# Four graph layers in one kernel: how the first layer is planned beside an eigenvector computation, and how the second layer's instructions are kept in order

## The chip, the cores and the metric

The kernel runs on one NeuronCore of a Trainium2 chip. The metric is the device time of one execution in microseconds (us). Times are medians of several runs; the profile is one execution more, whose own time is given beside it. The engines that matter are TensorE (PE, matmuls; PEld is its weight load), VectorE (DVE), ScalarE (ACT) and SyncE (SP), which issues the DMAs.

## What is computed

`x` has 128 graphs of 64 nodes with 256 features; `adj` is one 64 x 64 adjacency matrix. Each of four layers computes `h = relu(layernorm(x))` and adds the layer's output to `x`:

```python
# layer 0: h mixed with the normalized adjacency, two products, a batchnorm over all rows after each
agg = einsum('nm,bmd->bnd', A_hat, h)
t   = relu(batchnorm(agg @ W1.T + b1))          # 512 wide
x   = x + batchnorm(t @ W2.T + b2)              # 256 wide
# layer 1: the same with the eigenvectors of the normalized Laplacian
_, U = eigh(L_norm)
agg  = einsum('mn,bnd->bmd', U.T, h)
x    = x + einsum('nm,bmd->bnd', U, relu(agg @ W1 + b1) @ W2 + b2)
# layer 2: two graph convolutions with adj, then LSTMs over windows of 1, 2, 3 and 4 nodes
# layer 3: attention along 512 edges with a softmax per source node
```

Layers 2 and 3 are not touched by the change.

## The kernel before

**Tiles.** The 8192 rows of `x` lie in 16 blocks `X0` to `X15` of 512 rows each (128 partitions x 4 x 256). A block's layer norm takes four BATCH_NORM_STATS2, a short chain of small DVE operations with one square root on ACT, and four ACT activations (relu with scale and bias).

**Layer 0 beside the eigenvectors.** Layer 1 needs the eigenvectors `U` of a 64 x 64 matrix. They come from one long chain of small operations: 62 Householder steps that bring the matrix to tridiagonal form (`Fast.tridiagonal`, `Fast.householder`, one step per column c = 63 down to 2), then `Fast.vectors` (eigenvalues by polynomials, twisted factorizations, a verdict whether the result is good). Layer 0 is independent of it and runs beside it. `Plan` decides the order: `chain` places a step of the long chain as soon as its inputs are there by the planner's costs; `beside` puts a step of layer 0 into a queue per engine, and `fill` places queued steps in the time that an engine waits for the next chain step, if they fit with a little slack (0.6 us on T, 0.3 on S and V, for TensorE, ScalarE and VectorE). `emit` then issues all in the planned order, and with `nc.ordered` each instruction is tied behind the one before it on its engine (class `Ordered`; the ties cost no semaphores). What is not tied is put in order by the framework's own list scheduler, by its estimates, and it can be moved across a long stretch of the program.

**Layer 0's steps** (`hidden0`, `hidden_block`, `features0`). For each block: norm, relu (4 on ACT), two mixes (8 matmuls each with the block-diagonal `BDH`, tile `z`), eight products with W1 into four PSUM banks; each bank is read twice, by a BATCH_NORM_STATS2 into `st` and by an ACT copy that keeps the hidden values. When all 16 blocks are through, four BATCH_NORM_AGGREGATE (`bn_mv`) and a chain of small operations (`affine`) give scale and shift. Then for each block four ACT relus (tile `z`), eight products with W2, an ACT copy with a sum (into `big`) and an ACT square with a sum. The sums give the second batchnorm (tiles `bn_a`, `bn_b`, `bn_sh`, `bn_sc`). The norms of blocks 0 to 3 are computed together as one chain of 16 statistics and 13 small operations (`norms`), and so on by fours. The first of them wait in the plan for `came`, four empty chain steps on T that stand for the arrival of X0 to X3.

**DMAs of the start.** SP issues, in this order: adj and its transpose, X0 to X15, the weights and biases of layer 1 (`weights1`, tiles `w`, `w_n`, `w_b`), W1 and W2 of layer 0 and its six vectors. Then each Householder step issues one small DMA that copies the row `f_x` into a row of `f_V` (in `row_uk`). `f_x` has four buffers; a step cannot write a buffer before that DMA of four steps ago has read it.

**From layer 0 to layer 1** (`eigenvectors`). After the plan: three block-diagonal matrices from `U`, its transpose and adj (`block_diagonal`; tiles `BDU`, `BDUT`, `BDA`); for blocks 0 and 1 `end0`, which applies the second batchnorm (two ACT activations on `big`), transposes (8 on PE, PSUM tiles `ps` or `pe`) and adds to X (two DVE additions); the norm factors of block 0 (`norm0`, tiles `n_st`, `n_mv`, `n_v`, `n_r`, `n_m`); then a value is loaded on every engine, and a conditional branch skips a slow eigenvector routine that runs only where the verdict is bad.

**Layer 1** (`layer1`). For each block i: `first` (16 matmul records and a DVE maximum, tile `g`), `second` of block i - 1 (two DVE additions `y`, one into X), `mixed_again` (8, an ACT copy), `mixed` of block i + 1 (16; the copies `a` by DVE and ACT), `end0` of block i + 3, the norm of block i + 2 (tile `h`). None of this is tied before the change. `N1` (tile `w_n`) is the negative of a bias, made once by a DVE operation.

The code below has the lines of the profile; most compute instructions carry line 799, as they are issued through `Ordered`, so the profile is read by the tiles' names.

Of the kernel before, what the change touches and what calls it, by code (L numbers as in the profile page):

```python
# [787 lines left out]
class Ordered:  # L788
# [6 lines left out]
    def __getattr__(self, name):  # L795
        method = getattr(self.engine, name)

        def call(*a, **kw):
            i = method(*a, **kw)  # L799
            behind = self.last if self.owner.ordered else self.hold  # L800
            if behind is not None:
                self.owner.tc.add_manual_dep(i.ins, behind.ins.name, mybir.DependencyInfo(
                    mybir.DependencyClass.NoSync, mybir.DependencyReason.DATA), reason="issue order")
            if self.hold is None:
                self.last = i
            return i

        return call


class Engines:
# [5 lines left out]

    def __getattr__(self, name):
        return getattr(self.nc, name)


class Step:
# [3 lines left out]
    def __init__(self, engine, emit, needs, busy, ready, bank):  # L826
        self.engine, self.emit, self.needs = engine, emit, needs
        self.busy, self.ready, self.bank = busy, ready, bank
        self.at = None


class Plan:
# [26 lines left out]
    def fill(self, engine, until):  # L859
        while True:  # L860
            best = None
            for x in self.queue[engine][:12]:
                at = self.start(x)
                if at is not None and at + x.busy <= until + self.slack[engine] and (best is None or at < best[0]):
                    best = at, x
            if best is None:
                return
            self.queue[engine].remove(best[1])
            self.place(best[1], best[0])
# [7 lines left out]
    def beside(self, engine, emit, needs=(), busy=0.1, ready=0.22, bank=None):  # L877
        x = Step(engine, emit, needs, busy, ready, bank)
        self.queue[engine].append(x)
        return x  # L880
# [14 lines left out]
class Fast:  # L895
# [7 lines left out]
    def __init__(self, tc, ctx, k):  # L903
        self.tc, self.nc, self.k = tc, k.nc, k
        self.o = Ops(k.nc)
        self.pool = ctx.enter_context(tc.tile_pool(name="fast", bufs=1))
        self.rows = ctx.enter_context(tc.tile_pool(name="fastr", bufs=3))
        self.ps = ctx.enter_context(tc.tile_pool(name="fastps", bufs=2, space=PSUM))
        self.psv = ctx.enter_context(tc.tile_pool(name="fastvps", bufs=1, space=PSUM))
        self.tiles = {}  # L910
# [74 lines left out]
    def tridiagonal(self, S, made, plan):  # L985
# [24 lines left out]
        def first():  # L1010
            x = now["x"] = self.rows.tile([64, 65], F32, name="f_x", bufs=4)
            o.copy(x[:, 0:63], now["p"][:, 0:63])
# [10 lines left out]
    def householder(self, c, now, go, row, h, rest, scalars, square):  # L1023
# [40 lines left out]
        def row_x():  # L1064
            now["x"] = self.rows.tile([64, 65], F32, name="f_x", bufs=4)
            o.stt(x(0, w), now["uk"][:, 0:w], now["v"][:, w:c], now["z"][:, 0:w], ALU.mult, ALU.add)
# [123 lines left out]
    def values(self):  # L1190
# [5 lines left out]
        def signs(s):  # L1196
            if s % 4 == 3:
                SG = self.SG = self.rows.tile([128, 4, 64], F32, name="f_SG")
# [248 lines left out]
class Kernel:  # L1447
# [39 lines left out]
    def begin(self):  # L1487
# [9 lines left out]
        for i in range(NB):  # L1497
            self.X.append(self.c(f"X{i}", P, TPB, D))
            self.load_x(i)
# [5 lines left out]
    def block_diagonal(self, bd, M, psum):  # L1505

        p = psum.tile([P, N], F32, name="ps")
# [70 lines left out]
    def eigenvectors(self):  # L1578
# [3 lines left out]
        with ExitStack() as ex:  # L1582
# [10 lines left out]
            left = fast.vectors(self.U[:], self.UT[:])  # L1593
            plan.rest()
            plan.emit()
            for bd, M in ((self.BDU, self.U), (self.BDUT, self.UT), (self.BDA, self.AT)):
                self.block_diagonal(bd, M[:], self.ps0)
            for i in range(2):
                self.end0(i, self.ps0, "ps")
            self.norm0 = self.factors(self.w0, 0, self.const)  # L1600
            bad = nc.values_load(left[0:1, 0:1], min_val=0, max_val=64)
# [45 lines left out]
    def norms(self, pool, blocks):  # L1647
# [4 lines left out]
        st = pool.tile([P, n, 6], F32, name="m_st")  # L1652
        d, v, y, r, m = (pool.tile([P, n], F32, name="m_" + x) for x in "dvyrm")
# [50 lines left out]
    def affine(self, pool, tag, mean, var, b, g, be):  # L1704
# [5 lines left out]
            ("S", lambda: self.act(y[:], v[:], AF.Sqrt)),  # L1710
            ("V", lambda: o.recip(r[:], y[:])),
# [3 lines left out]
            ("V", lambda: o.ts(sc[:], r[:], 2.0, ALU.mult)),  # L1715
            ("V", lambda: o.mul(sc[:], sc[:], g[:])),
            ("V", lambda: o.add(v[:], mean, b[:])),
            ("V", lambda: o.sub(sh[:], b[:], v[:])),
# [22 lines left out]
    def open0(self, ctx):  # L1741
# [4 lines left out]
        self.W0 = self.weights(w, "w0_1", io["L0_gnn_W1_t"]), self.weights(w, "w0_2", io["L0_gnn_W2_t"])  # L1746
        self.v0 = [self.columns(w, "w0_" + n, io["L0_gnn_" + n]) for n in "b1 g1 be1 b2 g2 be2".split()]
        self.st1 = w.tile([P, 4, NB, 6], F32, name="st1")
        self.sums = w.tile([P, 2, 2, NB], F32, name="sums")

# [6 lines left out]
    def hidden0(self, plan, mixes):  # L1757

        nc, pool, psum, W1 = self.nc, self.p0, self.ps0, self.W0[0]
        beside, used, banks = plan.beside, {}, []  # L1760
        for i in range(NB):
            if i % 4 == 0:
                r, m, steps = self.norms(pool, range(i, i + 4))
                came = [plan.chain("T", lambda: None, (), 0.0, 5.5 + 1.5 * (i + k)) for k in range(4)] if i == 0 else []
                d = []
                for n, (engine, emit) in enumerate(steps):
                    if n < 4 * TPB:
                        d.append(beside("V", emit, [came[n // TPB]] if came else [], 0.36, 0.45))
                    else:
                        d = [beside(engine, emit, d, 0.12, 0.25)]  # L1770
                normed = d
            banks += self.hidden_block(i, r, m, plan, normed + used.get(i - 3, []) + [mixes], used)
        self.features0(plan, banks, used)

    def hidden_block(self, i, r, m, plan, needs, used):
# [3 lines left out]
        def relu(j):  # L1779
            if j == 0:  # L1780
                now["z"] = pool.tile([P, 4, BT], F32, name="z", bufs=3)
                now["h"] = now["z"][:, 0:2, :].rearrange("p c (t d) -> p (c t) d", d=D)
            self.act(now["h"][:, j, :], self.X[i][:, j, :], AF.Relu, scale=r[:, i % 4, j:j + 1],
                     bias=m[:, i % 4, j:j + 1])
# [20 lines left out]
        for hc in range(4):  # L1805
# [5 lines left out]
                               0.62, 0.7))  # L1811
# [5 lines left out]
    def features0(self, plan, made, used):  # L1817
# [7 lines left out]
        def sequence(steps, d):  # L1825
            for engine, emit in steps:
                d = [beside(engine, emit, d, 0.12, 0.25)]
# [3 lines left out]
        d = [beside("V", lambda j=j: nc.vector.bn_aggr(mv[:, j, :], flat(self.st1[:, j, :, :])), made, 0.5, 0.65)  # L1831
# [66 lines left out]
    def end0(self, i, psum, name="pe"):  # L1898

        sc2, sh2 = self.affine2  # L1900
        for oc in range(2):
            self.act(self.part(i, oc), self.part(i, oc), AF.Identity, scale=sc2[:, oc:oc + 1], bias=sh2[:, oc:oc + 1])
        self.add_transposed(psum, i, lambda dc, j: self.part(i, dc)[:, j * P:(j + 1) * P], name)
# [22 lines left out]
    def layer1(self, pool, psum, ps2, ps0, tables, after):  # L1926
        o = self.o
        (W1, W2), N1, b1, T = self.W1, self.N1, self.b1, self.T1

# [32 lines left out]
        mixed(0)  # L1962
        self.end0(2, ps0)
        hs[1] = self.norm(pool, 1)
        o.ts(N1[:], N1[:], -1.0, ALU.mult)
        for i in range(NB + 1):
# [20 lines left out]
            if i + 2 < NB:  # L1987
                hs[i + 2] = self.norm(pool, i + 2)
            if i == NB - 1:
                after()  # L1990
# [34 lines left out]
    def layer2(self, pool, psum, ps2, ps0):  # L2025
# [26 lines left out]
        def block(i):  # L2052
            if i == 2:
                with ExitStack() as ce:
                    epool = ce.enter_context(self.tc.tile_pool(name="l3e", bufs=1, side="right"))
                    nc.vector.hold, nc.scalar.hold, nc.tensor.hold = nc.vector.last, nc.scalar.last, nc.tensor.last
                    self.edges(self.w3, epool, ps0)
                    nc.vector.hold = nc.scalar.hold = nc.tensor.hold = None
# [476 lines left out]
    def run(self):  # L2535
# [4 lines left out]
        with cx:  # L2540
            self.big = [pool.tile([P, 2, 4 * BT], F32, name="big") for pool in pools]
            with ExitStack() as ex:
                self.weights1(ex.enter_context(self.tc.tile_pool(name="l1c", bufs=1)))
# [47 lines left out]
```

## Time and profile before

| | us |
|---|---|
| median of three runs | 2362.17 (2361.97 to 2363.38) |
| the profiled execution, its own time | 2361.27 |
| its span from the first to the last instruction | 2359.5 |
| stage of layer 0 and the eigenvectors, to the start of the second batchnorm's chain | 0 to 388.9 |
| from there to the first relu of layer 1 | 388.9 to 405.4 |
| layer 1, to the first mix of layer 2 | 405.4 to 519.6 |
| layers 2 and 3 | 519.6 to 2359.5 |

Engines over the whole span: PE 97% busy, DVE 68%, ACT 48%. The busy shares are sums of instruction durations; neighbouring DVE or ACT instructions overlap a little, and PE's ends are modelled, so PE can be shown busy while it runs at half its clock. A timeline line gives the start, the duration, engine, operation, output and inputs, and, in brackets, how long the engine was idle before and for whom.

### The profile page before, as it was taken

What the parts mean: (1) busy time and instruction counts of PE and PEld (TensorE: products, weight loads), DVE (VectorE), ACT (ScalarE), POOL (GpSimd) and SP (SyncE); (2) the same over time, 40 slices, a digit from 0 to 9 for tenths busy, and PEclk for the clock granted to TensorE, in tenths of its full rate; (3) what the DMA queues carried; (4) which work ended last, traced back from release to release, by engine and by line L of the source; (5) the groups of instructions that cost most, each with busy time, mean ns of one, the idle gap of its engine ahead of it and who ended that gap; (6) DMA issues with size and microseconds to landing.
All of it is one profiled execution on the core that took longest, in us unless ns stands there. A gap on an engine that the chain in (4) does not pass through costs nothing.

```text
span 2359.5 us, 32444 instructions
## 1 busy us (share of the span) xinstructions
PE 2281.3 (97%) x12061; PEld 1618.5 (69%) x12061; DVE 1603.2 (68%) x4045; ACT 1134.5 (48%) x2488; POOL 2.9 (0%) x26
## 2 busy tenths in 40 slices
PE   5998997999999999999999999999999999999989
PEld 3554344997777788888999998888884444444434
DVE  5887675999437786666777676559655566556467
ACT  4665766544436654434444444336445544344321
POOL 0000000000000000000000000000000000000000
PEclk9999999999999999999999999999999999999989
DMA  5000221131010000000000002000020000000001
GB/s 169 1 1 1 63 63 36 65 81 36 1 36 1 1 18 1 1 1 32 6 1 1 1 1 72 1 1 16 1 63 10 1 5 19 14 14 19 14 14 50
DMA packets 61194, 54.88 MB, mean 23 GB/s; under 512 B 15203, under 2 KB 58852, under 8 KB 61028
## 3 DMA queue, kind: packets, MB, share of 16 engines
q1 hardware_dynamic: 61028, 52.73, 7.3%
q8 instruction: 97, 1.59, 0.3%
q14 instruction: 69, 0.57, 0.1%
HBM read 35.93 MB, written 16.78 MB: 22 GB/s over the span
## 4 chain that ended last, share of the span: by engine, by line
PE 78%; DVE 3%; ACT 1%; issue 1%; DMA 0%; ACTq 0%; DVEq 0%
PE ps L799 68%; PE acc L799 5%; PE pt L799 4%; PE y L799 1%; PE pe L799 1%; DVE sm_m L799 1%; DVE X L799 1%; ACT ls_g L799 0%; ACT big L799 0%; DVE aw L799 0%; ACT L799 0%; DVE n_st L799 0%; DMA ls_w<-in_L_gnn_Wih_t_dram 0%; ACT h L799 0%; DVE sm_e L799 0%
## 5 line engine op out<-in xcount | busy, mean ns | idle before, releaser
L799 ACT ACTIVATE ls_g<-ls_g,ls_b 128x512 f32<-128x512 f32 (+4 forms) x472 | 243.0, 565 | 153.6 <-DVE ls_g L799 151.8
L799 ACT ACTIVATE ls_g<-ps,ls_b 128x256 f32<-128x256 f32 (+3 forms) x268 | 115.3, 470 | 329.7 <-PE ps L799 326.5
L799 PE MATMUL ps<-z,w 128*128 128x512 f32 x512 | 256.1, 627 | 0.0
L799 PE MATMUL ps<-big,X 128*128 128x176 f32 (+3 forms) x848 | 212.9, 367 | 1.6 <-ACT big L799 1.5
L799 DVE TENSOR_TENSOR aw<-at,ed_OST 128x1024 f32<-128x1024 f32 x128 | 150.0, 1219 | 92.4 <-PE ps L799 92.4
L799 DVE TENSOR_TENSOR ls_g<-ls_z,ps 128x512 f32<-128x512 f32 (+5 forms) x256 | 146.8, 579 | 90.8 <-PE ps L799 89.3
L799 PE MATMUL ps<-ls_tx,X 128*128 128x160 f32 (+2 forms) x960 | 206.9, 327 | 0.6 <-ACT ls_g L799 0.6
L799 PE MATMUL ps<-X,X 128*128 128x160 f32 (+1 forms) x896 | 199.0, 306 | 0.0
L799 PE MATMUL ps<-X,ls_w 128*128 128x256 f32 x640 | 190.5, 379 | 0.0
L799 PEld LDWEIGHTS ps<-ls_tx,X 128*128 128x128 f32 x960 | 161.8, 190 | 15.0 <-DVE X L799 4.7
L799 PEld LDWEIGHTS ps<-big,X 128*128 128x128 f32 x848 | 146.0, 190 | 31.4 <-issue 19.4
L799 DVE TENSOR_TENSOR X<-ls_g 128x1024 f32<-128x1024 f32 (+2 forms) x108 | 117.4, 1087 | 50.5 <-ACT ls_g L799 50.4
L799 ACT ACTIVATE r<-ps 128x512 f32<-128x512 f32 x256 | 129.3, 625 | 41.1 <-PE ps L799 41.0
L799 PEld LDWEIGHTS ps<-X,X 128*128 128x128 f32 x896 | 148.5, 190 | 0.0
L799 PE MATMUL ps<-X,ls_s 128*128 128x256 f32 x480 | 142.3, 379 | 0.0
L799 PEld LDWEIGHTS ps<-z,w 128*128 128x128 f32 x512 | 89.2, 193 | 72.9 <-issue 64.6
L799 PE MATMUL ps<-ls_tx,ls_s 128*128 128x256 f32 x464 | 134.8, 379 | 0.0
L799 PE MATMUL ps<-ls_tx,ls_w 128*128 128x256 f32 x464 | 133.4, 380 | 0.1
L799 PEld LDWEIGHTS ps<-X,ls_w 128*128 128x128 f32 x640 | 121.6, 190 | 16.6 <-DVE X L799 0.3
L799 PE MATMUL ps<-big,ls_w 128*128 128x256 f32 x464 | 132.0, 380 | 0.7 <-ACT ls_z L799 0.7
L799 PE MATMUL ps<-ed_S,Q 64*128 64x512 f32 x512 | 128.6, 617 | 0.5 <-DVE XV L799 0.3
L799 ACT ACTIVATE big<-ps 128x512 f32<-128x512 f32 x96 | 69.2, 749 | 113.8 <-PE ps L799 113.6
(534 smaller groups left out, 4024.3 us busy)
## 6 DMA issues: line engine op xcount, KB each, us to landing
X<-in_x_dram SPq DMA_DIRECT2D x32, 512.0 KB
xs<-X SPq DMA_DIRECT2D x16, 512.0 KB
X<-xs SPq DMA_DIRECT2D x16, 512.0 KB
out_dram<-X SPq DMA_DIRECT2D x32, 256.0 KB
X<-in_L_gnn_Wih_t_dram SPq DMA_DIRECT2D x4, 512.0 KB
ls_w<-in_L_gnn_Wih_t_dram SPq DMA_DIRECT2D x4, 512.0 KB
ls_w<-in_L_gnn_Whh_t_dram SPq DMA_DIRECT2D x4, 512.0 KB
w<-in_L_gnn_W_t_dram SPq DMA_DIRECT2D x2, 512.0 KB
```

The lines of the kernel that those rows point to most:

```text
L799: i = method(*a, **kw)
```

## The change

It touches the stage of layer 0 and the eigenvectors, the passage to layer 1, and the order in layer 1.

- **DMAs.** X0 is loaded first, then layer 0's W1, X1 to X15, W2 and the vectors; layer 1's constants come last of the loads.
- **Block 0's norm by itself.** The norms are computed for blocks 0, 1 to 3, and then by fours. `came` is now an `event` with a time of its own instead of a chain step on T. The steps of block 0's norm are `urgent`: `fill` prefers such a step and places it as soon as it could start before the next chain step, whether it fits or not.
- **Batchnorm chains.** The first batchnorm's statistics of blocks 14 and 15, its aggregates and its chain are urgent; `affine` has one operation fewer, and two are moved beside the square root.
- **Buffers.** `f_x` has eight buffers; the pool's other tiles two in place of three.
- **Passage.** The block-diagonal matrices are emitted before the rest of the plan, in another PSUM tile; the value is loaded before the second batchnorm is applied; the scalings of blocks 0 and 1, the transposes and `norm0` are tied in an order with `norm0` ahead of block 1's additions.
- **Layer 1.** Everything up to the end of its first iteration is tied in program order (the negation of N1 too). After that, instructions of an iteration are only held behind what was last on their engine when the iteration before began.

```diff
 class Engines:
+    def fresh(self):
+        for e in (self.tensor, self.vector, self.scalar):
+            e.last = None
+    def mark(self):
+        return [e.last for e in (self.tensor, self.vector, self.scalar)]
+    def hold(self, marks=(None, None, None)):
+        for e, last in zip((self.tensor, self.vector, self.scalar), marks):
+            e.hold = last
...
     def fill(self, engine, until):
...
-                if at is not None and at + x.busy <= until + self.slack[engine] and (best is None or at < best[0]):
-                    best = at, x
+                if at is not None and (at + x.busy <= until + self.slack[engine] or x.urgent and at <= until):
+                    if best is None or (not x.urgent, at) < best[:2]:
+                        best = not x.urgent, at, x
...
+    def event(self, at):
+        x = Step(None, None, (), 0.0, at, None)
+        x.at = 0.0
         return x
...
-        self.rows = ctx.enter_context(tc.tile_pool(name="fastr", bufs=3))
+        self.rows = ctx.enter_context(tc.tile_pool(name="fastr", bufs=2))
...
-            x = now["x"] = self.rows.tile([64, 65], F32, name="f_x", bufs=4)
+            x = now["x"] = self.rows.tile([64, 65], F32, name="f_x", bufs=8)
...
             self.X.append(self.c(f"X{i}", P, TPB, D))
-            self.load_x(i)
+        self.load_x(0)
...
             left = fast.vectors(self.U[:], self.UT[:])
+            for bd, M in ((self.BDA, self.AT), (self.BDU, self.U), (self.BDUT, self.UT)):
+                self.block_diagonal(bd, M[:], fast.psv, "fvps")
             plan.rest()
             plan.emit()
-            for bd, M in ((self.BDU, self.U), (self.BDUT, self.UT), (self.BDA, self.AT)):
-                self.block_diagonal(bd, M[:], self.ps0)
+            bad = nc.values_load(left[0:1, 0:1], min_val=0, max_val=64)
+            nc.ordered = True
             for i in range(2):
-                self.end0(i, self.ps0, "ps")
-            self.norm0 = self.factors(self.w0, 0, self.const)
-            bad = nc.values_load(left[0:1, 0:1], min_val=0, max_val=64)
+                self.features1(i)
+            for i in range(2):
+                self.add_transposed(self.ps0, i, lambda dc, j, i=i: self.part(i, dc)[:, j * P:(j + 1) * P], "ps")
+                if i == 0:
+                    self.norm0 = self.factors(self.w0, 0, self.const)
+            nc.ordered = False
+        nc.fresh()
...
             ("S", lambda: self.act(y[:], v[:], AF.Sqrt)),
+            ("V", lambda: o.add(sh[:], mean, b[:])),
+            ("V", lambda: o.sub(sh[:], b[:], sh[:])),
...
-            ("V", lambda: o.ts(sc[:], r[:], 2.0, ALU.mult)),
-            ("V", lambda: o.mul(sc[:], sc[:], g[:])),
-            ("V", lambda: o.add(v[:], mean, b[:])),
-            ("V", lambda: o.sub(sh[:], b[:], v[:])),
+            ("V", lambda: o.stt(sc[:], r[:], 2.0, g[:], ALU.mult, ALU.mult)),
...
-        self.W0 = self.weights(w, "w0_1", io["L0_gnn_W1_t"]), self.weights(w, "w0_2", io["L0_gnn_W2_t"])
+        W1 = self.weights(w, "w0_1", io["L0_gnn_W1_t"])
+        for i in range(1, NB):
+            self.load_x(i)
+        self.W0 = W1, self.weights(w, "w0_2", io["L0_gnn_W2_t"])
...
+        self.weights1(self.consts1)
...
     def hidden0(self, plan, mixes):
-                r, m, steps = self.norms(pool, range(i, i + 4))
-                came = [plan.chain("T", lambda: None, (), 0.0, 5.5 + 1.5 * (i + k)) for k in range(4)] if i == 0 else []
+        for lo, hi in ((0, 1), (1, 4), (4, 8), (8, 12), (12, 16)):
+            r, m, steps = self.norms(pool, range(lo, hi))
+            came = [plan.event(4.5 + 1.5 * (i + (i > 0))) for i in range(lo, min(hi, 4))]
...
+                    d.append(plan.beside(engine, emit, [came[n // TPB]] if came else [], 0.36, 0.45, urgent=not lo))
+                else:
+                    d = [plan.beside(engine, emit, d, 0.12, 0.25, urgent=not lo)]
...
             bank.append(beside("V", lambda hc=hc: nc.vector.bn_stats(self.st1[:, hc, i, :], now["p", hc][:]), [x],
-                               0.62, 0.7))
+                               0.62, 0.7, urgent=i >= NB - 2))
...
-                d = [beside(engine, emit, d, 0.12, 0.25)]
+                d = [beside(engine, emit, d, 0.12, 0.25, urgent=True)]
...
     def layer1(self, pool, psum, ps2, ps0, tables, after):
+        nc.fresh()
+        nc.ordered = True
...
         mixed(0)
+        o.ts(N1[:], N1[:], -1.0, ALU.mult)
         self.end0(2, ps0)
         hs[1] = self.norm(pool, 1)
-        o.ts(N1[:], N1[:], -1.0, ALU.mult)
+        marks = nc.mark()
         for i in range(NB + 1):
...
+            nc.ordered = False
+            nc.hold(marks)
+            marks = nc.mark()
             if i == NB - 1:
+                nc.hold()
                 after()
```

## Prediction, made before the change was built or run

> **What bounds the kernel now.** I read the windows first: busy time of each engine by stretch (start:end, length, then PE, PEld, DVE, ACT, POOL with instruction counts, PE clock, DMA share, GB/s).
>
> ```profile
> 12.00:38.00 26.00, 7.06 (x40) 5.67 (x40) 14.74 (x81) 7.45 (x33) 0.00 (x0) 1.00 0.90 271
> 38.00:227.00 189.00, 185.45 (x859) 97.49 (x857) 148.54 (x727) 124.70 (x425) 0.00 (x0) 1.00 0.01 1
> 227.00:240.60 13.60, 3.34 (x36) 2.67 (x36) 12.14 (x71) 5.39 (x28) 0.00 (x0) 0.62 0.01 1
> 279.00:370.00 91.00, 88.27 (x302) 39.57 (x302) 69.40 (x333) 60.30 (x147) 0.00 (x0) 1.00 0.19 55
> 406.50:520.00 113.50, 111.92 (x851) 105.15 (x850) 106.85 (x354) 62.03 (x126) 0.00 (x0) 1.00 0.22 68
> ```
>
> From 38 us on PE sets the pace of layer 0, except for a hole at 227 to 240.6; before 38 it is all but idle. In layer 1 PE and DVE are both full. So layer 0 gains by an earlier start of PE, a smaller hole, and a shorter passage to layer 1. The timeline says what holds the start, first on DVE, then on PE:
>
> ```profile
> 27.14 0.21 DVE L799 SCALAR_TENSOR_TENSOR f_junk<-f_uA,f_uk 64x60 f32<-64x60 f32 x1 [0.39 <-ACT f_uk L799]
> 30.43 0.23 DVE L799 TENSOR_SCALAR w_n<-w_n 128x128 f32<-128x128 f32 x1 [3.08 <-DMA w_n<-in_L_gnn_b_dram]
> 36.78 0.27 DVE L799 SCALAR_TENSOR_TENSOR f_x<-f_uk,f_v,f_z 64x59 f32<-64x59 f32 x1 [5.94 <-DMA f_V<-f_x]
> ...
> 31.54 2.08 PE L799 MATMUL ps<-BDH,z 128*128 128x128 f32 x8
> 38.15 2.07 PE L799 MATMUL ps<-BDH,z 128*128 128x128 f32 x8
> 40.73 2.08 PE L799 MATMUL ps<-z,w 128*128 128x512 f32 x2
> ```
>
> At step c = 60 DVE waits twice: for layer 1's bias, whose negation was put in here, and for an `f_x` buffer whose copying DMA stands in SP's queue behind all loads (SP issues the first at 34.78). PE's order is fixed, so the second mix stands behind the stalled step. Then the hole and the passage:
>
> ```profile
> 229.35 0.68 DVE L799 BATCH_NORM_STATS2 st<-ps 128x6 f32<-128x512 f32 x1
> 235.91 0.57 DVE L799 BATCH_NORM_AGGREGATE bn_mv<-st 128x2 f32<-128x96 f32 x1
> 239.75 1.51 ACT L799 ACTIVATE z<-X,bn_sh,bn_sc 128x512 f32<-128x512 f32 x2
> 240.63 2.08 PE L799 MATMUL ps<-z,w 128*128 128x512 f32 x2
> ...
> 385.87 0.22 ACT L799 ACTIVATION_READ_ACCUMULATOR ps<-ps,bn_less 128x1 f32 x1
> 388.93 0.18 DVE L799 TENSOR_REDUCE bn_a<-sums 128x2 f32<-128x32 f32 x1 [2.96 <-DVEq L1602]
> 405.37 2.08 ACT L799 ACTIVATE h<-X,n_m,n_r 128x256 f32<-128x256 f32 x4
> ```
>
> The four aggregates come one per Householder step. After the last square DVE waits 2.96 us for its branch, and layer 1's first relu comes 16.4 us after the second batchnorm starts. The verdict itself was ready at 369.7 (CAST at 369.55), 14.5 us before PE's last product ended (384.24).
>
> [...] a mix takes 2.08 us at 31.54 and 1.16 at 214.11; after the hole the low clock lasts 6.4 us (0.50 in 240.6 to 247). [...] `f_v` waited behind the bias. [...] the branch itself is 0.07 us on DVE, but its next event comes 2.9 us later. I use 2.96.
>
> **The change, part by part**, against the profiled execution's 2361.27 us; the median is 0.90 above it.
>
> *The stall.* With N1's negation tied into layer 1 and eight buffers, both waits go: 3.08 + 5.94 and the two operations between, 36.78 - 27.35 = 9.4 us of the chain. What is late next: the ninth write of `f_x`, at c = 55, needs the DMA of c = 63. That still stands behind the same bytes (landing about 36.8), and c = 55 comes at about 50 (57.79 less about 7). Cover 13 us; if it is gone, it costs its excess. The pool's two buffers in place of three wait for readers one whole step back, so 0.
>
> *SP's queue.* The same loads in another order. W1 is now second behind X0; X1 to X3 move 0.5 MB back, 1.5 us at about 330 GB/s. Layer 1's constants go last; they are needed after 360. Cost 0.
>
> *Block 0's norm.* By the planner's own costs, the old `came` counts from when T is free (6.3 after the adjacency's steps): block 3 at 6.3 + 5.5 + 4.5 = 16.3, four statistics 1.9 and 13 operations of 0.25 bring the first relu to 21.5. It ran at 25.78, 4.3 later than planned; the first `f_x` was planned at 8.9 and ran at 11.25, 2.4 later. New: statistics from 6.7 in the chain's waits, ready at 8.9, 3.3 for the chain: 12.2, so really 14.6 to 16.5; I take 15. Relus need 3 us (25.78 to 28.6 before), so the first mix runs at about 17.5 in place of 31.54, and the first product at 22 in place of 40.73. I take **19 us** for PE's stream. Blocks 1 to 3 need 12 statistics and 13 operations; 16 and 13 took 11.3 us (14.39 to 25.7), so they are ready at about 23, before block 0's products end. Cost to the chain: four 0.34 and 12 of about 0.1, half of it in waits: 1.2 us.
>
> *The hole.* From the last hidden product (226.6) to 240.63: 14 us. With urgent steps: two statistics 1.4, four aggregates 2.2, eleven chain operations 2.4 and the root, one relu 0.8, woven with chain steps: 8. Gain **6 us**. `affine`'s fewer operation: 0.2, once in each batchnorm.
>
> *Where the two meet.* PE's last product: 384.2 - 19 - 6 = 359.2; but features now lie beside 14 Householder steps in place of 9, and each has about 0.9 us of its own matmuls: + 4.5 = 363.7. The chain: 369.7 - 9.4 + 1.2, and two steps that lay in the hole (3.3 us each) now lie under load (4.1): 1.6. Verdict at 363.1. They meet; squares end 1.9 after PE: 365.6; branch on DVE 363.1 + 3.0 = 366.1. So the second batchnorm starts at 366.1 in place of 388.9: **-22.8**, -23.0 with `affine`. On PE and ACT the branch lies in their remaining work; PE's branch took 3.5 us before without a gap in its matmuls. Bounds: 0 if ACT and PE carry their branches in the queue, + 3 if one is exposed. I take 0.
>
> *Passage.* Before, ACT ran 11 scalings and DVE 11 additions for blocks up to 7 ahead of block 0's relu. Tied: two scalings 1.55, transposes and two additions to + 3.9, statistics 1.4, aggregates 0.4, root and six operations 1.8: relu at + 7.5 after the batchnorm's chain, in place of 12.9 (405.37 - 392.49): **-5.4**.
>
> *Layer 1.* The work that ran ahead (5.5 blocks of transposes, 44 x 0.109 = 4.8 us of PE, 11 additions of 0.6 = 6.6 us of DVE) returns into a loop where both are full. Also in the tied first iteration `first` needs `a`, `mixed_again` needs `g`, and `g` stands on DVE behind block 1's norm (3.3 us), for which block 0's mix and PE wait. Less one block's, which stays ahead: **+ 5.4**, between 0 and + 9. The loop's pace was 7.0 us per block (113.5 / 16 = 7.1); a hold of one to two iterations still leaves the engines a block of freedom: 0, bounded by -3 (fewer waits at DVE) and + 8 (0.5 us a block).
>
> Sum: -23.0 - 5.4 + 5.4 = -23.0; 2361.27 - 23.0 = 2338.3, as a median **2339.2**.
>
> **Rivals.**
> *A, forecast: 2339* (2331 to 2347), 0.55.
> *B, the chain is the later one or PE starts less early: 2348.* If block 0's relu comes only where DVE's stall was (PE -9.4 us), the hole gives 3 and the branch 2.96 hides: -15 + 1 = -14. For: the plan's times are rough (2.4 to 4.3 us off already at the start), and loaded steps last 4.2 us against 3.3 unloaded. Against: X0 lands long before it is used. 0.17.
> *C, the passage is paid back less, or the hole shrinks more: 2331.* -5.4 stays and layer 1 costs 0, with 3 more from its DVE: -31. For: DVE is what layer 1 waits for at its end (relu waits of ACT for `n_m` of about 4 us a block). 0.16.
> *D, slower: layer 1's order costs more than the rest gains.* If, in the held iterations, `g` stands behind the norm of a later block on DVE as in the tied one, PE waits once per block. It decides from 23 / 15 = 1.5 us a block; at 2.2 us a block it is + 33: 2372. For: DVE has 106.85 busy us in 113.5, so a wait is not caught up. Against: only the first iteration is fully tied. 0.07.
> *E, the change doesn't do what it says: 2359.* The stall moves to the next wait (X, `f_V`) and PE starts where it did; only the branch gains. 0.05.
>
> **Numbers.** About 0.2%, 4.7 us, is what a measurement can tell from no change. Faster: A, B, C and nearly half of E: 0.90; within: 0.03; slower: D: 0.07. Range: from C's 2331 less 4 for its own spread to B's 2348 plus 5: 2327 to 2353; outside lie D, E and tails, 0.2.
>
> **What would show it.** No DVE wait for `w_n` or `f_V` before 60 us; the first mix at about 17.5; first features product at about 216; `bn_a` at about 366; first relu of layer 1 7.5 us after the batchnorm's chain; layer 1 from its first relu to layer 2's first mix 119 to 120 us in place of 114. Wrong if the verdict comes later than 368, if PE waits in 20 to 60 us, or if layer 1's blocks take more than 7.5 us.

## The result, and the profile after

| us | before | after |
|---|---|---|
| median of 16 runs | 2361.62 (2360.14 to 2363.38) | 2354.26 (2350.15 to 2358.75) |
| ratio, 95% interval | | 0.9971 [0.9964, 0.9979] |
| profiled execution, its own time | 2361.27 | 2354.39 |
| second batchnorm starts (`bn_a`) | 388.9 | 368.7 |
| its chain ends (`bn_sh`) | 392.5 | 375.5 |
| first relu of layer 1 (`h`) | 405.4 | 383.05 |
| first mix of layer 2, called the third layer below | 519.5 | 514.0 |
| from `bn_a` to that mix | 130.6 | 145.3 |

The kernel is 7.4 us faster; 23 were forecast, and the time lies 1.3 us above the stated range. By the two profiles the first stage gives 20.2 us, and the stretch from the second batchnorm to the third layer takes 14.7 of them back. The windows of the kernel after (start:end, length, then PE, PEld, DVE, ACT, POOL with counts, PE clock, DMA share, GB/s):

```profile
12.00:38.00 26.00, 21.95 (x99) 13.77 (x98) 21.78 (x114) 17.98 (x60) 0.00 (x0) 1.00 0.91 267
38.00:207.90 169.90, 166.39 (x775) 86.48 (x773) 134.30 (x653) 109.90 (x378) 0.00 (x0) 0.99 0.01 2
207.90:217.00 9.10, 1.91 (x22) 1.45 (x21) 7.49 (x44) 3.72 (x17) 0.00 (x0) 0.75 0.00 0
217.00:368.00 151.00, 147.16 (x513) 63.48 (x513) 102.00 (x537) 102.25 (x296) 0.00 (x0) 0.97 0.21 56
384.10:514.00 129.90, 123.02 (x888) 115.36 (x889) 112.14 (x365) 72.17 (x143) 0.00 (x0) 0.95 0.19 60
```

The first 26 us now hold 21.95 us of PE's work (7.06 before), and the hole is 9.1 us (13.6). In layer 1 DVE is busy 86% of its window, where it was 94%. The timeline after, at the places shown for before:

```profile
17.05 3.98 PE L799 MATMUL ps<-BDH,z 128*128 128x128 f32 x16 [0.58 <-ACT z L799]
22.20 4.56 PE L799 MATMUL ps<-z,w 128*128 128x512 f32 x10
...
209.57 0.57 DVE L799 BATCH_NORM_AGGREGATE bn_mv<-st 128x2 f32<-128x96 f32 x1
217.00 1.22 PE L799 MATMUL ps<-z,w 128*128 128x512 f32 x1 [0.76 <-ACT z L799]
...
369.89 0.17 DVE L799 TENSOR_SCALAR bn_b<-bn_b 128x2 f32<-128x2 f32 x1
373.69 0.17 DVE L799 TENSOR_SCALAR bn_v<-bn_b 128x2 f32<-128x2 f32 x1 [3.63 <-DVEq L1626]
...
383.05 2.07 ACT L799 ACTIVATE h<-X,n_m,n_r 128x256 f32<-128x256 f32 x4 [1.45 <-DVE n_m L799]
```

DVE has no wait for `w_n` or `f_V` before 60 us. The first product comes 18.5 us earlier, the first features product 23.6. But the jump over the slow eigenvector code, which stood ahead of `bn_a`, now stands inside the chain, between `bn_b` and `bn_v`: 3.63 us. The instructions of the conditional's line (count, shortest/median/longest ns, first and last start) say how long each engine jumps:

```profile
L1626 ACTq EVENT_SEMAPHORE  x2: 17/17/17, 371.8 to 371.9; - x2
L1626 DVEq EVENT_SEMAPHORE  x2: 21/21/21, 373.5 to 373.6; - x2
L1626 ACTq COMPARE_BRANCH  x1: 50/50/50, 368.9 to 368.9; - x1
L1626 PEldq COMPARE_BRANCH  x1: 4012/4012/4012, 368.9 to 368.9; - x1
L1626 DVEq COMPARE_BRANCH  x1: 72/72/72, 370.5 to 370.5; - x1
```

DVE branches at 370.5 in 72 ns and goes on at 373.5; ACT needs 2.9 us (368.9 to 371.8), PE 4.0. On DVE and ACT the branch record is the small part of it (72 and 50 ns) and a gap behind it the rest; on PE the record itself lasts 4012 ns.

**The loss in layer 1.** From the batchnorm's end to the third layer's first mix, one window of each kernel, before and after:

```profile
392.50:519.50 127.00, 121.81 (x904) 112.43 (x905) 117.38 (x382) 75.56 (x146) 0.74 (x3) 0.98 0.19 62
```
```profile
375.50:514.00 138.50, 126.60 (x904) 118.42 (x905) 117.50 (x384) 76.35 (x149) 0.74 (x3) 0.94 0.19 60
```

DVE (the third pair) has the same work, 117.4 and 117.5 us, and is idle 9.6 and 21.0 us. With equal work the idle time must grow by what the window grows, 11.4 us; what counts is where it lies. By windows inside it, 16 of the 21 us lie in the first 34.5 us, up to 410 (first before, then after):

```profile
392.50:406.50 14.00, 10.39 (x60) 7.78 (x61) 11.03 (x31) 13.99 (x22) 0.74 (x3) 0.82 0.02 5
406.50:420.00 13.50, 11.99 (x96) 11.35 (x95) 13.23 (x65) 13.17 (x26) 0.00 (x0) 1.00 0.16 22
```
```profile
375.50:384.10 8.60, 3.58 (x16) 3.06 (x17) 5.36 (x19) 4.18 (x8) 0.74 (x3) 0.70 0.28 66
384.10:396.00 11.90, 8.59 (x40) 7.84 (x40) 5.27 (x20) 3.49 (x8) 0.00 (x0) 0.61 0.15 24
396.00:410.00 14.00, 12.24 (x79) 11.45 (x80) 7.78 (x24) 6.62 (x12) 0.00 (x0) 0.88 0.00 0
```

PE falls behind as well: in its first 34.5 us it has 135 of its 904 matmuls, where it had 209 before, and from 430 us on it is busy without a gap (from 420 before, but for 0.1 us). So both engines enter the rest of the layer with work undone, and these lines don't tell which of the two sets its length. The timeline of the tied first pass shows what they wait for:

```profile
384.12 3.76 PE L799 MATMUL ps<-BDU,h 128*128 128x128 f32 x16 [3.94 <-ACT h L799]
386.26 0.69 DVE L799 COPY a<-ps 128x512 f32<-128x512 f32 x1 [2.24 <-PE ps L799]
387.92 0.60 ACT L799 ACTIVATE a<-ps 128x512 f32<-128x512 f32 x1 [2.79 <-PE ps L799]
388.41 1.51 ACT L799 ACTIVATE big<-big,bn_sh,bn_sc 128x512 f32<-128x512 f32 x2
389.27 0.47 PE L799 MATMUL pe<-ident,big 128*128 128x128 f32 x1 [1.39 <-ACT big L799]
390.91 0.69 DVE L799 TENSOR_TENSOR X<-X,pe 128x512 f32<-128x512 f32 x1 [3.82 <-PE pe L799]
...
395.63 0.68 DVE L799 TENSOR_TENSOR g<-ps,w_n 128x512 f32<-128x512 f32 x1
396.36 1.76 PE L799 MATMUL ps<-BDUT,g 128*128 128x128 f32 x8 [2.03 <-DVE g L799]
```

It is one chain: ACT scales block 2 only behind its copy `a`, which waits for the mix; PE waits for the scaling, DVE for PE's transposes (3.82 us), and then `g`, behind block 1's norm on DVE, keeps PE waiting (2.03).

### The profile page after: what moved, and what is told of

The parts are those of the page before. It is cut to its first block, busy times and chain, and to the rows that moved or that the text cites. A ratio compares the mean times of both kernels' runs of the same rounds, so it can differ in the third digit from the quotient of the medians.

```text
span 2352.6 us, 32457 instructions
## 1 busy us (share of the span) xinstructions
PE 2285.1 (97%) x12061; PEld 1620.8 (69%) x12061; DVE 1604.6 (68%) x4055; ACT 1134.0 (48%) x2489; POOL 3.0 (0%) x26
## 4 chain that ended last, share of the span: by engine, by line
PE 79%; DVE 3%; ACT 1%; issue 1%; ACTq 0%; DVEq 0%
PE ps L799 68%; PE acc L799 5%; PE pt L799 4%; PE pe L799 1%; PE y L799 1%; DVE X L799 1%; DVE sm_m L799 1%; ACT ls_g L799 0%; DVE n_st L799 0%; DVE aw L799 0%; ACT L799 0%; ACT big L799 0%; ACT h L799 0%; DVE sm_e L799 0%; DVE ls_g L799 0%
## 5 line engine op out<-in xcount | busy, mean ns | idle before, releaser
L799 DVE TENSOR_TENSOR X<-ls_g 128x1024 f32<-128x1024 f32 (+2 forms) x108 | 117.5, 1088 | 50.5 <-ACT ls_g L799 50.4
L799 PE MATMUL ps<-X,ls_s 128*128 128x256 f32 x480 | 142.3, 379 | 0.0
L799 ACT ACTIVATE h<-X,n_m,n_r 128x256 f32<-128x256 f32 x192 | 99.7, 589 | 45.8 <-DVE n_m L799 22.4
```

## The experiments

Theory: from the second batchnorm on, DVE's work is the length of the stretch; the tied first pass leaves it idle, since no later block's transposes and norm can fill the holes. Rivals: the hold of the later blocks; a low PE clock (0.61 in the window from 384.1, and PE had stood 3.94 us just before); the jump. The table has each kernel's median and, from its trace, `bn_a` and the stretch from there to the third layer's first mix. That stretch compares kernels well: what happens before `bn_a` varies by some us between runs of the same code (last section), while the stretch is 143.2 to 145.4 us in the kernel after and in the four that differ from it only in the first stage or the hold. Medians are of 5 runs, other counts in brackets.

| kernel | median us | ratio to before, 95% | `bn_a` | `bn_a` to third layer |
|---|---|---|---|---|
| after (16) | 2354.3 | 0.9971 [0.9964, 0.9979] | 368.7 | 145.3 |
| no_hold | 2352.4 | 0.9957 [0.9944, 0.9971] | 367.1 | 145.0 |
| free_layer | 2347.3 | 0.9939 [0.9925, 0.9952] | 370.8 | 134.8 |
| hold_only | 2345.4 | 0.9932 [0.9918, 0.9946] | 367.3 | 134.0 |
| free_all | 2339.3 | 0.9918 [0.9904, 0.9932] | 367.1 | 133.2 |
| hold_late_n | 2342.7 | 0.9918 [0.9905, 0.9932] | 373.5 | 133.5 |
| free_late_n | 2344.2 | 0.9920 [0.9907, 0.9934] | 373.5 | 133.5 |
| late_branch | 2346.1 | 0.9937 [0.9924, 0.9951] | 376.4 | 133.7 |
| late_branch_n | 2343.0 | 0.9922 [0.9908, 0.9935] | 367.0 | 134.2 |
| no_branch | 2350.5 | 0.9952 [0.9939, 0.9966] | 364.2 | 139.4 |
| no_branch_n (4) | 2337.6 | 0.9902 [0.9887, 0.9917] | 368.1 | 129.4 |
| prefill | 2350.7 | 0.9953 [0.9939, 0.9966] | 370.8 | 139.3 |
| tied_all | 2401.0 | 1.0158 [1.0144, 1.0172] | 368.9 | 194.1 |
| before_tied | 2372.4 | 1.0047 [1.0033, 1.0061] | 388.5 | 142.3 |
| four_bufs (13) | 2362.7 | 1.0004 [0.9996, 1.0012] | 379.2 | 145.4 |
| four_norm (21) | 2359.5 | 0.9992 [0.9985, 0.9999] | 378.2 | 143.2 |
| no_urgent (6) | 2354.3 | 0.9966 [0.9954, 0.9978] | 372.1 | 143.9 |

### Which tie costs: free_layer, no_hold, hold_only

```diff
 # hold_only: the first pass isn't tied
         nc.fresh()
-        nc.ordered = True
 # no_hold: the first pass tied, no hold after it
             nc.ordered = False
-            nc.hold(marks)
-            marks = nc.mark()
 # free_layer: both
```

> The kernel after with the two ordering edits of the second layer taken back: its first pass isn't tied and no engine is held within a block. Theory (starved VectorE): from the end of the second batchnorm to the first mix of the third layer VectorE has the same 117.4 us of work in both kernels, and it stood idle 9.6 us of it before and 21.0 us after, because the tied order keeps the next blocks' transposes and norms from filling the holes. Untied, the idle time goes back to about 10 us: the first BDA mix of the third layer comes at about 503 (514.0 after) and the time at about 2343. Rival (cold clock): the stage is longer because TensorE begins it after a longer pause at 0.6 of its clock, whatever the order; then the mix stays at 512 to 514 and the time at 2352 to 2354.

> The kernel after with the tied passage and first pass kept, and only the hold of the later blocks taken away. Theory (starved VectorE): 16 of the 21 idle us lie in the first 35 us, in the tied part, so the hold costs nearly nothing: the time stays within 2 us of 2354. Rival (the hold itself makes each block wait for the last): the idle time goes and the time falls to about 2343.

> The kernel after with the second layer's first pass untied, but the later blocks still held within a block. Theory (starved VectorE in the tied first pass): most of the 11 us comes back, 2343 to 2347. Rival (the hold): 2354, no gain.

Untying the first pass takes 11.3 us off the stretch and 8.9 off the time; dropping the hold takes 0.3 and 1.9, and there the intervals of the ratios overlap. From the batchnorm's end to the third layer `hold_only` has:

```profile
374.10:501.30 127.20, 122.30 (x904) 116.44 (x905) 117.31 (x384) 75.89 (x149) 0.74 (x3) 0.96 0.20 65
```

The hold is free; the tied first pass is the cost. The edit frees the negation too, which moves to 36.6 us; `hold_late_n` below, where it stays tied, has the same short stretch. The low clock falls as a rival: without the jump (`no_branch` below) the tied pass takes 136.2 us from the batchnorm's end, 10.2 of them at half clock (0.50, counted in windows of 1 us), while the free pass of `hold_late_n` takes 126.7 with 14.1 at half clock.

### The same edits on the kernel before: before_tied

Layer 1's order alone (tied first pass, hold, tied negation), put into the kernel before.

> The kernel before with the second layer's edits alone: its first pass tied, the later blocks held, the negation of N1 tied into it. Theory (the tied first pass starves VectorE and loses the blocks that had run ahead): the time from the second batchnorm's end to the third layer's first mix grows from 127 to about 136 to 138 us, and the whole to about 2370 to 2373. Rival (the loss comes only with the earlier start, where TensorE is cold or data is late): no slower than 2364.

10.8 us slower than the kernel before, and the stretch grows by 11.7. So the loss doesn't need the earlier start. A second reading: with the negation tied away, the 3.08 us wait for `w_n` is gone, and the wait for `f_V` is 9.2 us in place of 5.94. Both ended on the same queue of loads; taking away the first alone gives nothing (`bn_a` at 388.5 for 388.9).

### Filling the holes, and tying all: prefill, tied_all

```diff
 # prefill: block 2 goes through the passage with blocks 0 and 1
-            for i in range(2):
+            for i in range(3):
                 self.features1(i)
-            for i in range(2):
+            for i in range(3):
                 self.add_transposed(...)
...
-        self.end0(2, ps0)
 # tied_all: tied through the last block
-            nc.ordered = False
-            nc.hold(marks)
-            marks = nc.mark()
             if i == NB - 1:
-                nc.hold()
+                nc.ordered = False
```

> The kernel after, all ties kept, but with block 2's scaling, transposes and additions moved by hand ahead of block 0's relu, into the holes where ScalarE, TensorE and VectorE stand. Theory (what is missing in the holes is work for VectorE, not freedom as such): VectorE's idle time falls by 3 to 4 us, and the time to about 2350.5. Rival (the later blocks in the tied pass set the pace whatever is done ahead): 2353 to 2355.

> The kernel after with the whole second layer tied in program order, not only its first pass. Theory (the loss lies in the start, where nothing has been done ahead; in the loop the program order already has three blocks in flight): 0 to 0.3 us a block more, 2354 to 2359. Rival (a tied order costs in every block what it costs in the first, some 8 us or at least 1.5 us, as the prediction's slower case has it): 2375 or more.

With the ties kept and one block's work moved into the holes, 3.6 us of the time and 6.0 of the stretch come back. So about half of the 11.3 us is work that was missing, whatever the ties. In `tied_all` the theory fell and its rival came true: 46.7 us slower. The stretch is 48.8 us longer, over the 15 later blocks 3.3 us a block. Its waits in 385 to 560 (engine, tile, releaser: us, times, longest), those of PE and then DVE:

```profile
PE pe L799 <- ACT big L799: 25.2, 28, 1.4
PE ps L799 <- DVE g L799: 12.1, 9, 2.2
```
```profile
DVE X L799 <- PE pe L799: 39.1, 17, 3.8
DVE a L799 <- PE ps L799: 6.0, 2, 3.8
```

These are the waits of the first pass above, again and again: DVE waits 17 times for PE's transposes, PE nine times for `g`. The program order of a block makes three engines wait in a ring, as in the timeline above, where ACT's scaling (388.41) stands behind its copy `a` (387.92), which had waited 2.79 us for the mix. The wait for `g` is the mechanism of the prediction's slower rival, and the wait for the transposes is larger; the change has both in one pass and not in the loop.

### The passage: free_all, free_late_n, hold_late_n

```diff
 # free_all: hold_only, and the passage untied
-            nc.ordered = True
             for i in range(2):
                 self.features1(i)
 # hold_late_n: hold_only; free_late_n: free_all; both with
+            self.o.ts(self.N1[:], self.N1[:], -1.0, ALU.mult)   # tied behind the second batchnorm
...
-        o.ts(N1[:], N1[:], -1.0, ALU.mult)
```

> The kernel with the first pass untied and the hold kept (the run with 2345.4), and now also the passage untied: scalings, transposes and norm of blocks 0 and 1 are no longer in an order of their own. The prediction counted 5.4 us for that order, since block 0's relu comes earlier. Theory (VectorE's work is what the stretch from the batchnorm to the third layer is made of, so an earlier relu buys nothing where VectorE is busy either way): within 1.5 us of 2345.4. Rival (the prediction's passage step): 5 us slower, 2350 to 2351.

> The same with the passage tied. Theory (VectorE is the bound from the second batchnorm on, an earlier relu buys nothing): within 1.5 us of the one with the passage free. Prediction's passage step: 5.4 us faster than it. Third reading (the order itself costs, as the runs at 2345.4 and 2339.3 suggest): 5 us slower.

> First pass and passage untied, hold kept, and the negation of the second layer's bias tied behind the second batchnorm's chain on VectorE, so that it cannot drift back to where its load lands. Theory (the wait for that load was part of the runs' spread): no wait for w_n before 60 us, 2338 to 2340, with fewer runs at 2345. Rival (the spread comes from elsewhere, such as the clock's grants): the same two groups, 2339 and 2345.

By the medians `free_all` is 6 us faster than `hold_only`, against both expectations; but its five runs lie apart (three at 2339.1 to 2339.3, two at 2344.7 and 2345.5), and its stretch is only 0.8 shorter. The profiles of `hold_late_n` and `free_late_n` have the same clock in each window up to 205 us, and `bn_a` at 373.5 in both. Here they are from the batchnorm's end to the third layer:

```profile
380.30:507.00 126.70, 122.01 (x905) 116.06 (x906) 117.37 (x384) 75.96 (x149) 0.74 (x3) 0.95 0.20 66
```
```profile
380.40:507.00 126.60, 122.14 (x905) 114.91 (x906) 116.84 (x384) 75.90 (x149) 0.74 (x3) 0.96 0.20 66
```

With the passage tied block 0's relu comes at 387.9, without at 390.2: 2.3 us earlier, and the third layer begins at 507.0 in both. The earlier relu buys nothing. DVE has 117.4 and 116.8 us of work, PE 122.0 and 122.1, and in `hold_late_n` PE has no gap from 414.8 on; whether DVE's work or PE's sets the length is not shown. With the negation tied the runs still spread, from 2339.1 to 2345.3 in `free_late_n`, so the wait for `w_n` isn't the cause of that.

### The jump: no_branch, late_branch, late_branch_n, no_branch_n

```diff
 # no_branch (of after), no_branch_n (of free_late_n)
-            bad = nc.values_load(left[0:1, 0:1], min_val=0, max_val=64)
...
-        with self.tc.If(bad > 0):
...
 # late_branch (of hold_only), late_branch_n (of hold_late_n)
+            nc.ordered = True
+            o.copy(late[:], left[:])
-            bad = nc.values_load(left[0:1, 0:1], min_val=0, max_val=64)
+            bad = nc.values_load(late[0:1, 0:1], min_val=0, max_val=64)
```

> The kernel after without the If and the general eigenvector code under it, which the data of this case never enters (the reading of the verdict goes too). Theory (the jump stands in the batchnorm's chain): VectorE's 3.6 us wait ahead of bn_v goes, the first scaling of the features comes at about 371.9 instead of 375.5, and the time falls by 3 to 4 us to about 2350.5. Rival (hidden, as the prediction took it): the chain waits for something else that comes as late, and the time stays at 2354.

> As free_late_n, without the If and the code under it, which this data never enters. Theory (VectorE's 3.6 us in the batchnorm's chain are on the path whatever follows): 3 to 4 us faster than free_late_n, 2335 to 2336. Rival (the free layer takes up the delay): within 1 us of it.

> The same kernel (first pass untied, hold kept), with the verdict copied once more on VectorE after the second batchnorm's chain, and loaded from that copy, so that the jump no longer stands in the chain. Without any jump the time fell 3.8 us. Theory (VectorE's wait inside the chain is what the jump costs): the chain ends 3.6 us earlier, VectorE jumps while it would wait for the first transposes, 2 to 3 us gained, about 2343. Rival (the jump costs on whichever engine it stands ahead of needed work): TensorE now waits for the copy and jumps for 4 us ahead of the first transposes, which come no earlier: 2345 to 2346.

> As hold_late_n, with the verdict copied once more behind the batchnorm's chain and loaded from the copy, so that the jump comes after the chain. Theory (the jump costs what it costs on whichever engine it stands ahead of needed work; here TensorE's, ahead of the first transposes): within 1 us of hold_late_n. Rival (its place in VectorE's chain is what costs): 2 to 3 us faster.

Without the jump the time falls by 3.8 us, and by 6.6 where the layer is free; the intervals of the ratios overlap a little, but the traces agree: the stretch is 5.9 and 4.1 us shorter, and in `no_branch` the chain from `bn_a` takes 3.2 us in place of 6.7. (The edit also takes out the code that is jumped over.) So the jump is on the path: the prediction's "0" was wrong. The time of `late_branch` can't be read, since in its profile the negation had drifted to 37.9 and waited 3.7 us for its load; its stretch is that of `hold_only`. `late_branch_n` has no such wait: the jump left DVE's chain, and nothing was gained (134.2 against 133.5). Its timeline:

```profile
369.99 0.16 DVE L799 TENSOR_TENSOR bn_sh<-bn_sh,w_be 128x2 f32<-128x2 f32 x1
370.07 0.14 DVE L799 COPY late<-f_k_badi 64x1 int32<-64x1 int32 x1
374.13 5.04 ACT L799 ACTIVATE big<-big,bn_sh,bn_sc 128x512 f32<-128x512 f32 x7 [3.14 <-ACTq L1630]
375.60 3.27 PE L799 MATMUL ps<-ident,big 128*128 128x128 f32 x16 [9.23 <-PEq L1630]
376.73 0.69 DVE L799 TENSOR_TENSOR X<-X,ps 128x512 f32<-128x512 f32 x1 [6.39 <-PE ps L799]
```

The chain ends 3.6 us sooner, and then ACT and PE jump ahead of the scaling and the transposes, and DVE waits for them 6.39 us (2.54 in the kernel after).

### The first stage: four_bufs, four_norm, no_urgent

```diff
 # four_bufs, in two places
-            x = now["x"] = self.rows.tile([64, 65], F32, name="f_x", bufs=8)
+            x = now["x"] = self.rows.tile([64, 65], F32, name="f_x", bufs=4)
 # four_norm
-        for lo, hi in ((0, 1), (1, 4), (4, 8), (8, 12), (12, 16)):
+        for lo, hi in ((0, 4), (4, 8), (8, 12), (12, 16)):
 # four_norm: no "urgent" in the norms; no_urgent: none in the batchnorms
-                               0.62, 0.7, urgent=i >= NB - 2))
+                               0.62, 0.7))
...
```

> The kernel after with four f_x buffers again in place of eight. Theory (the stall for the DMA comes back at c = 59 or 58, until about 36.8, and TensorE, whose order is fixed, stands with it): VectorE waits 4 to 8 us before 40, and the stage and the time grow by 4 to 8 us, to about 2360. Rival (only the eigenvector chain stalls, which has time to spare until the verdict): less than 2 us.

> The kernel after with the norms of blocks 0 to 3 again as one chain, not urgent; arrival times as after. Theory (TensorE's early start comes from block 0's norm by itself, and the end of the stage follows TensorE's stream): the first mix comes at about 25 in place of 17, the second batchnorm 6 to 8 us later, and of that nearly all is in the end: about 2361. Rival (the eigenvector chain is the later one): the second batchnorm moves by less than 2 us, 2355.

> The kernel after without urgent steps in the two batchnorm chains (block 0's norm stays urgent). Theory (TensorE's stream sets the end of the stage): the hole between the last hidden product and the first features product grows from 9 back to about 14 us, and the time by 4 to 5, to about 2359. Rival (chain steps that the urgent work pushes back cost as much): 2353 to 2355.

The first undoes the whole gain, the second most of it: + 8.4 and + 5.2 us. `four_bufs` has PE's first mix at 17.2 as after, then this wait on DVE, and in 30 to 45 us PE does 7.65 us of work at a mean clock of 0.66, where the kernel after has 14.25 at 1.00:

```profile
DVE f_x L799 <- DMA f_V<-f_x: 8.2, 1, 8.2
```
```profile
30.00:45.00 15.00, 7.65 (x36) 5.01 (x34) 5.05 (x25) 5.63 (x19) 0.00 (x0) 0.66 0.27 49
```

`four_norm` has the first mix at 24.5 and `bn_a` 9.5 us later. `no_urgent` went as its rival said: the first features relu comes 4.7 us later (220.8), as the theory expected, but the verdict comes 2.5 us sooner (365.6) and `bn_a` 3.4 later, so DVE and PE jump (at 366.4) beside PE's last products, and only ACT's jump (371.6) stands ahead of its last square, for 2.19 us. The chain from `bn_a` takes 5.4 us in place of 6.7. The third layer begins 2.0 later, less than profiles of one first stage differ by, and the median doesn't move. In these two profiles the larger hole is in part paid for by a jump that is partly hidden.

## Why the prediction was wrong

Its own sum against the profiled execution:

| step | predicted us | measured us | miss |
|---|---|---|---|
| second batchnorm starts | 366.1 | 368.7 | + 2.6 |
| its chain | 3.4 | 6.7 | + 3.3 |
| then block 0's relu | 7.5 | 7.6 | + 0.1 |
| from there to the third layer | 119.5 | 131.0 | + 11.5 |
| the rest | as before, 1840.0 | 1838.6 | - 1.4 |

Together + 16.1: from 2338.3 to 2354.4, each 1.8 us above its sum of steps, since the steps make up the span and the execution's own time is 1.8 longer.

- **The stall, SP's queue, block 0's norm: right.** First mix 17.05 (17.5 predicted), first product 22.2 (22), no wait of DVE for a load. `four_bufs` and `four_norm` show both steps carry the gain.
- **The hole: right in kind, smaller.** 9.1 us for 8, first features product at 217.0 for 216. Its worth may be less than that: the prediction added it to the sum whole, while a shorter hole also brings PE's last product up to the verdict and uncovers the jump (`no_urgent`: 4.7 us of hole, 2.0 at the third layer, nothing in the median).
- **Where the two meet: right, late.** Verdict at 368.1 and PE's end at 367.9, for 363.1 and 363.7. From the first features product to PE's end it is 150.9 us, where the prediction's own numbers give 147.7 and before had 143.6. Of the 7.3 more, 3.9 are the W2 products (128.7 us for 124.8; the half clock lasts 9 us there in place of 6.4, and half of these 2.6 us, an estimated 1.3 by the last section's pair of products, 2.08 us at 0.50 and 1.12 at 1.00, is its part), 3.1 the other matmuls that lie there now. `bn_a` is at 367.0 to 367.3 in four kernels with the same first stage and jump that ran less at half clock (last section), so about 1.5 of the 2.6 us belong to this run.
- **The branch: wrong,** its own upper end, + 3, was right. The prediction's 366.1 has DVE's jump in it (363.1 + 3.0), nearly all of it beside squares that were to end at 365.6, and it took 0 for PE and ACT, whose jumps were to lie in their remaining work. But the verdict came with the last product (in all eleven kernels with this first stage and no stall 0.6 us before `bn_a`), so no work was left to lie beside, and DVE's jump stood inside the chain. The first two rows of the table belong together for this reason: + 5.9.
- **The passage, -5.4: wrong in worth.** The relu came when it said (7.6 us), and that is worth nothing (`hold_late_n` against `free_late_n`). The work of DVE and PE stays, in whatever order.
- **Layer 1, "+ 5.4, between 0 and + 9": the step that failed.** It saw the wait of `g` behind the norm in the tied pass and counted the work that returns. With the passage its terms add up to 0, and that is what comes with the first pass free (`hold_only`: 127.2 us from the batchnorm's end, 127.0 before). In the tied pass it is 138.5: from block 0's relu to the third layer + 16.9 us over before, beyond its upper end. What the term lacked is the ring of waits: ACT's scaling behind its copy, PE's transposes behind the scaling, DVE's additions behind the transposes, with no other block's work to fill them, + 11.4 us of idle time on DVE. The hold's pace, taken at 0, was right (0.3 us of the stretch).

## What to carry over

Where engines are busy most of a stretch, count their work and their idle time over the whole stretch, from one event to another. A step that comes earlier inside it need not be a gain, and a tie is judged by the idle time it leaves. Before tying the program order of a block, follow the first pass over the engines by hand: if each waits once for the next, keep a block of work ahead of it, or leave that pass free. With the first pass free and the rest of the change kept, the medians are 2345.4 and, with the negation tied elsewhere, 2342.7 us (`hold_only`, `hold_late_n`), ratio 0.993 and 0.992 to before: more than twice the gain of the change as it stands.

## Not expected of the hardware

- **The jump.** Over the untaken body ACT stands 2.9, DVE 3.0 and PE 4.0 us in the kernel after, while the branch record of ACT and DVE takes 0.05 and 0.07. Moving it from one engine's chain to another's didn't help; where PE's last products lay beside it (`no_urgent`) the chain was 1.3 us shorter. Why it takes so long no run shows.
- **The granted clock differs from run to run.** The 16 runs after the change spread over 8.6 us, those before over 3.2. One stretch of the profiles of `free_all` and then of `free_late_n` shows how (the clock is the third number from the end):

```profile
120.00:160.00 40.00, 40.00 (x181) 20.30 (x181) 32.12 (x159) 25.55 (x88) 0.00 (x0) 1.00 0.01 1
```
```profile
120.00:160.00 40.00, 40.00 (x173) 20.58 (x173) 30.28 (x149) 23.75 (x81) 0.00 (x0) 0.94 0.01 1
```

The 0.94 is a mean. In windows of 0.25 us the clock is 0.50 from 117.6 to 124.4 and 1.00 behind that. PE had stood 1.15 us for a Householder step just before; in `free_all` it stood 1.16 us at the same step, and the clock stayed at 1.00. The same two products behind that wait:

```profile
118.06 0.24 PE L799 MATMUL fps<-f_v,f_uk 1*41 1x41 f32 x2 [1.16 <-DVE f_v L799]
118.31 1.12 PE L799 MATMUL ps<-z,w 128*128 128x512 f32 x2
```
```profile
117.48 0.24 PE L799 MATMUL fps<-f_v,f_uk 1*41 1x41 f32 x2 [1.15 <-DVE f_v L799]
117.75 2.08 PE L799 MATMUL ps<-z,w 128*128 128x512 f32 x2
```

A second spell follows at 203.0, behind a wait of 1.41 us. The two last 6.8 and 3.4 us, and half of that, an estimated 5.1 us by the two products above, is most of the 6.4 by which its `bn_a` is later. In the kernel after the spells up to 232 us last 3.4 us (from 198.8) and 13.7 us (from 212.3). By the mean clocks of windows up to 240 us, PE ran at half clock for an estimated 10 us in the five kernels with this first stage and no stall where `bn_a` comes at 364.2 to 367.3 (`no_branch`, `late_branch_n`, `no_hold`, `free_all`, `hold_only`), 17 us in `no_branch_n` and the kernel after, where it comes at 368.1 and 368.7, and 24 us in `hold_late_n` and `free_late_n`, where it comes at 373.5. Why the clock falls behind this wait in one run and not in the other stays open.
